# Layer 3's keys and values lead by eight tiles; expert weights and int8 weights are asked for later

## The chip, the cores and the metric

The kernel runs on one core of one Trainium2 chip. The metric is the device time of one launch in microseconds (us); less is better. A core has five engines with instruction streams of their own: PE (TensorE, the matmuls), DVE (VectorE), ACT (ScalarE), POOL (GpSimd) and SP (SyncE, which here issues most transfers). Each engine works through its own stream in order; where it needs another's result it waits on a semaphore. Transfers are issued on queues of SP, ACT or POOL and carried out by the core's 16 DMA engines.

## The reference

Four layers follow each other on x of 32 x 64 x 512 (float32), that is 2048 rows or 16 tiles of 128 rows. Each layer is `x = x + ffn(cond(x))`.

- Layer 0: every pair of 64 rows is multiplied by a matrix chosen by an index; then latent attention and a mixture of experts, one shared and 7 routed, two for each row.
- Layer 1: again a matrix chosen by an index, then a mixture of 32 experts, four for each row.
- Layer 2: a low-rank adapter chosen by an index, then a soft mixture of experts.
- Layer 3: attention against a paged cache, then an int8-quantised linear layer.

The change concerns the start of the experts in layers 0 and 1, and layer 3. In short, for layer 3:

```python
q, k, v = x @ Wq.T, x @ Wk.T, x @ Wv.T          # 32 sequences of 64 rows, two to a tile
q, k = rope(rms(q)), rope(rms(k))               # positions from kv_lens
k_blocks, v_blocks = cache with the new k, v written at their positions
p = softmax(q @ k_all.T / 16, within a window of 256 behind each position)
y = (p @ v_all) @ Wo.T
out = int8(y) @ int8(weight).T * scales + bias  # scale per row of y, per row of weight
```

and for an expert in layer 0: `silu(x @ wg) * (x @ wu) / 8 @ wd`, added with the router's weights.

## The kernel before, in words

**How the order comes about.** The program is written out as Python that records instructions; a scheduling layer may reorder the instructions of an engine, except those that are recorded as to be kept in program order. `Prog.dma` keeps its transfers in program order unless told otherwise (`later=True` is its default, while `Prog.load` passes `later=False` unless asked). Gathers (`Prog.gather`, L284) are indirect transfers issued by POOL.

**Experts of layers 0 and 1 (`Moe`).** After routing, the rows of each expert stand in slots: `C` slots for each of `E` experts (640 slots and 7 experts in layer 0; 32 experts in layer 1). The work goes in units of 320 slots, two units to a pair of five row tiles. For each pair, `rows_of` gathers five row tiles `xr` on POOL, `turn` transposes them on PE (`tp`, L924), and then `into(u)` runs the gate and up matmuls (`gu`, L943: 128x128 weights against 320 columns), the activation, and `out_of(t)` the down matmul (`y`, L962) and the write of the result `ys` on SP. The weights of an expert are one transfer of 1536 or 1538 KB into one of three buffers (`weights(e)`, `wt`). Before unit u the weights for the expert of that unit and for the next two are asked for; before unit 0 only the first two. All these transfers are on SP's queue. Since they are kept in program order, but units are only an order of recording, the third expert's transfer stands on SP ahead of the first constants of layer 3.

**Beside the experts of layer 0** runs `layer3_ahead`, a generator whose steps are taken between the tiles of the experts (`Side`). Its first step loads layer 3's constants (480.5 KB), key lengths, the block table and the int8 weights (`w_i8`, 1024 KB, L213). Later steps work out the indices of cache rows, gather the cache rows, and quantise the weights.

**Layer 3.** `units` is a list of projections: `(1, t)` is the key and value projection of tile t (L1870, 8 matmuls of 128x512), `(0, t)` the query projection. Keys and values lead by `LAG` = 5 tiles. Queries 13 to 15 (`LAST` = 3) are not in the list: they are projected by `project` (L1924, L1928) inside the attention loop, 13 at step s = -3, 14 at s = -2, 15 at s = -1. Queries 11 and 12 are in the list but are only copied there (`qlate`) and normalised and rotated later, beside the attention, as are 13 to 15. For each other unit the length of each head is worked out (ACT `sq`, DVE `ss`, POOL `r` L1970), then the rotation (DVE `n`, `tc`, POOL `ts` L1988, DVE `qkv` L1997). A key/value tile is then written to `newkv` in memory (L1897 on SP); a query tile is transposed by `heads` (PE `tp`, L1844) into `qT`. The transposed rows `xT3` are kept in `LAG` + 3 buffers, since a query comes `LAG` tiles after its keys.

`old_rows` loads cached rows into 24 buffers `kvt`; `new_rows(b)` gathers the new key/value rows of sequence b over them (three gathers on POOL for each sequence, from `newkv`, L284). These wait until all of `newkv` is written. `Attend` then works in 64 steps s (four to a tile: two pairs of head groups, two sequences): `keys` transposes the keys of step s+3 (`kp`, L2021), `scores` runs step s+2 (`sp`, L2048), `turn0` and `turn1` transpose the softmax of step s (`pT`, L2070), `values` the product with the values (`op`, L2095). Between them `out` runs the output projection of finished tiles (`y`, L2117). The first eight sequences' gathers (24) fill the 24 buffers; a later sequence first needs its buffers free and its cached rows loaded again.

Of the kernel before, what the change touches and what calls it, by code (L numbers as in the profile page):

```python
# [20 lines left out]
P = 128  # L21
B, T, D = 32, 64, 512
NT = B * T // P
# [7 lines left out]
UNIT = 320  # L31
# [367 lines left out]
class Front:  # L399
# [43 lines left out]
    def weights(self, i):  # L443

        self.asked = self.g.cond_weights(self.sb, "wc0", self.at, i) if i < NT else None
# [235 lines left out]
class Moe:  # L681
# [25 lines left out]
        self.wp = ctx.enter_context(tc.tile_pool(name=f"ew{E}", bufs=3, reuse_waits="tile"))  # L707
        self.wts, self.bds = {}, {}

    def weights(self, e):  # L710
        if e < self.E and e not in self.wts:
            t = self.wp.tile([P, self.wlen], F32, name="wt")
            self.g.dma(t, self.g.a[self.wname][e * P : (e + 1) * P, :])
            self.wts[e] = t
        return self.wts.get(e)

# [193 lines left out]
    def run(self, xs, per_tile):  # L910
# [3 lines left out]
        with ExitStack() as ctx:  # L914
# [19 lines left out]
            def into(u):  # L934
                wg, wu, _, bias = self.parts(self.weights(u * UNIT // C))
                xT = xTs[u // 2][:, :, (u % 2) * UNIT : (u % 2 + 1) * UNIT]
                hT = sb.tile([P, 2, UNIT], F32, name="hT", bufs=3)
                for ic in range(2):
                    gu = []
                    for wj in (wg, wu):  # L940
                        o = ps.tile([P, UNIT], F32, name="gu", tag="gu", bufs=4)
                        for c in range(4):
                            nc.tensor.matmul(  # L943
                                o, wj[:, c, ic * P : (ic + 1) * P], xT[:, c, :], start=c == 0, stop=c == 3
                            )
                        gu.append(o)
                    self.act(g, sb, hT[:, ic, :], *gu, None if bias is None else bias[:, ic::2])
                hTs[u] = hT
# [30 lines left out]
            for u in range(units):  # L979
                p = u // 2  # L980
                if u % 2 == 0 and p + 1 < pairs:
                    self.rows_of(p + 1)
                for e in range(3):
                    if (u * UNIT // C + e) < E:
                        self.weights(u * UNIT // C + e) if u >= 1 or e < 2 else None
                into(u)
                self.bias_of(u * UNIT // C)

                if u % 2 == 0 and p > 0:
                    for j in (2, 3, 4):  # L990
                        out_of(5 * (p - 1) + j)
                if u % 2 == 1:
                    out_of(5 * p)
                    out_of(5 * p + 1)
                    if p + 1 < pairs:
                        turn(p + 1)
# [581 lines left out]
def layer3_ahead(g, pool, w):  # L1578
# [15 lines left out]
    nc.sync.dma_start(out=ki, in_=a["kvlen"].rearrange("o b -> b o"))  # L1594
    tab = sb.tile([B, NBLK], I32, name="tabi")
    nc.sync.dma_start(out=tab, in_=a["table"])
    wt = g.load(sb, "w_i8")
    yield

    w["ridx"] = ridx = sb.tile([P, NT], I32, name="ridx")  # L1600
# [29 lines left out]
    nc.vector.tensor_scalar(slots[:, 0:KB], iota[0:B, 0:KB], s0p, None, ALU.add)  # L1630
    nc.vector.tensor_scalar(slots[:, KB:], iota[0:B, 0:5], wsp, None, ALU.add)
    blk = sb.tile([B, KB + 5], F32, name="blk")
    yield
    for j in range(KB + 5):
        hot = sb.tile([B, NBLK], F32, name="hot3", bufs=2)
# [130 lines left out]
            yield  # L1766


LAG = 5
LAST = 3  # L1770


def layer3(g, w, xs, xb):
# [3 lines left out]
    with ExitStack() as ctx:  # L1777
# [36 lines left out]
        with ExitStack() as c1:  # L1814
# [38 lines left out]
            for u in range(len(units) + 5):  # L1853
# [10 lines left out]
                if u < len(units):  # L1864
                    z, i = units[u]
                    if z:
                        turn(i + 1)
                    pp = ps.tile([P, D], F32, name="pp3", tag="pp", bufs=5)
                    for c in range(4):
                        nc.tensor.matmul(  # L1870
                            pp, xT[i][:, c, :], (w["w_kv3"] if z else wq)[:, c, :], start=c == 0, stop=c == 3
                        )
                    late = not z and i >= NT - LAG
                    out = wp.tile([P, D], F32, name=f"qlate{i}") if late else sb.tile([P, D], F32, name="qkv3", bufs=6)
                    outs.append(out)
                    if late:

                        nc.scalar.copy(out, pp)
                        slow.append((i, out))
                        held.append(None)  # L1880
                    elif z:
                        nc.scalar.copy(out[:, 256:512], pp[:, 256:512])
                        held.append((pp, out, l3_length(g, sb, pp[:, 0:256])))
                    else:
                        held.append((pp, out, l3_length(g, sb, pp)))
# [51 lines left out]
        for s in range(-3, last + 8):  # L1937
            if s == -3:
                project(NT - LAST)
            if s % 2 == 0:  # L1940

                if s >= 4:
                    for _ in range(3):
                        old_rows()
                new_rows(s // 2 + 4)
            elif s == -3:
                new_rows(2)
            for stage, at in (("keys", s + 3), ("turn0", s), ("scores", s + 2), ("turn1", s)):
                if 0 <= at <= last:
                    getattr(f, stage)(at)  # L1950
            if -3 < s < LAST - 3:
                project(NT - LAST + s + 3)
            f.out()
            if s >= 2 and s % 2 == 0:
                next(beside, None)
            if 0 <= s - 1 <= last:
                f.values(s - 1)
# [222 lines left out]
```

## Time and profile before

| what | value |
|---|---|
| median of 3 runs | 2704.14 us (2700.83 to 2704.36) |
| the profiled execution: time | 2703.36 us |
| the profiled execution: span | 2701.6 us, mean granted PE clock 0.97 |
| PE busy | 2524.0 us (93%) |
| DVE, ACT, POOL busy | 1417.6, 725.6, 852.3 us |
| first gather of layer 0's experts | 409.16 us |
| first gather of layer 1's experts | 736.41 us |
| last key/value projection of layer 3 ends | 2380.5 us |
| first value product of layer 3 | 2431.34 us |

All times are on the axis of the profiled execution's span. A line of the timeline reads: start, duration, engine, source line, operation, tile written `<-` tiles read, sizes, `x` count of instructions drawn together, and in brackets the idle time before and what ended it. A line of waits reads: engine, line, `<-` what was waited for, total us, times, longest. In windows the columns are the stretch, its length, busy time of PE, PE's weight loads, DVE, ACT and POOL with counts, granted PE clock, busy share of the DMA engines, GB/s.

### The profile page before, as it was taken

To read this page: it belongs to the slowest core of one execution; us is meant where nothing else is said; L and a number is where in the kernel's file an instruction comes from. 1 tells how busy PE (TensorE), PEld (TensorE's weight loads), DVE (VectorE), ACT (ScalarE), POOL (GpSimd) and SP (SyncE) were. 2 spreads that over 40 slices of the span, in tenths; PEclk is the share of its full clock that TensorE was granted. 3 is DMA by queue.
4 is the path that set the end of the run, shared out by engine and by line. 5 is a ranking of instruction groups with operands and counts; after the bars stand their busy time and mean duration, and the time that the engine had idled before them with its cause. 6 is when DMAs were issued, how large, how long until landed. Compare 5 with 4: busy or idle time off the path is not lost.

```text
span 2701.6 us, 42326 instructions
## 1 busy us (share of the span) xinstructions
PE 2524.0 (93%) x16508; PEld 1620.7 (60%) x16523; DVE 1417.6 (52%) x3439; ACT 725.6 (27%) x1503; POOL 852.3 (32%) x904
## 2 busy tenths in 40 slices
PE   7999998996699999996999999999999999979998
PEld 5777775563565555564666666666666665435554
DVE  4666655643744444443544445555544431647886
ACT  2444430111311121110222222222222221236664
POOL 2222214623232233213233333333233321563440
PEclk9999989997699999998999999999999999989999
DMA  2333214445656976544122222222222223423441
GB/s 98 131 126 117 88 67 169 161 147 184 222 184 219 343 256 212 209 173 176 52 73 73 81 80 72 72 72 72 72 75 70 92 63 117 158 77 111 135 136 48
DMA packets 136213, 343.58 MB, mean 127 GB/s; under 512 B 24249, under 2 KB 25049, under 8 KB 128704
## 3 DMA queue, kind: packets, MB, share of 16 engines
q1 hardware_dynamic: 100368, 245.84, 26.3%
q0 software_dynamic: 35056, 89.13, 10.9%
q10 hardware_dynamic: 576, 5.77, 0.5%
q8 instruction: 134, 2.20, 0.3%
q14 instruction: 79, 0.65, 0.1%
HBM read 247.10 MB, written 109.58 MB: 132 GB/s over the span
## 4 chain that ended last, share of the span: by engine, by line
PE 41%; DVE 9%; issue 2%; DMA 1%; ACT 1%; POOL 0%; another core or an unknown queue 0%; SPq 0%; ACTq 0%; POOLq 0%; DVEq 0%
PE out L1557 8%; PE lp L1414 7%; PE pp L1870 3%; PE gp L1546 3%; PE zp L1491 3%; PE yp L1359 2%; PE y L2117 2%; PE hp L1523 2%; PE op L2095 2%; PE pT L2070 2%; PE sp L2048 2%; DVE xt L1025 1%; PE ep L1500 1%; DVE inv L1450 1%; PE kp L2021 1%
## 5 line engine op out<-in xcount | busy, mean ns | idle before, releaser
L943 PE MATMUL gu<-xT,wt 128*128 128x320 f32 x1472 | 408.5, 434 | 0.0
L943 PEld LDWEIGHTS gu<-xT,wt 128*128 128x128 f32 x1472 | 278.7, 191 | 123.4 <-issue 16.4
L1557 PE MATMUL out<-sb_w,gT 128*128 128x512 f32 x512 | 233.5, 599 | 10.7 <-DVE nn L1394 6.6
L962 PE MATMUL y<-wt,hT 128*128 128x512 f32 (+1 forms) x552 | 240.2, 608 | 0.2 <-DVE yo L971 0.2
L1414 PEld LDWEIGHTS lp<-xnT,sb_mu 128*128 128x128 f32 x2048 | 234.8, 193 | 9.2 <-issue 6.7
L1414 PE MATMUL lp<-xnT,sb_mu 128*128 128x128 f32 x2048 | 237.8, 276 | 2.1 <-ACT xnT L254 1.3
L1491 PE MATMUL zp<-sb_w,xnT 128*128 128x512 f32 x512 | 228.6, 595 | 5.1 <-DVE z L1493 5.1
L284 POOL DMA_INDIRECT kvst<-kv,gidx x96 | 97.7, 1017 | 271.6 <-DMA oldkv<-kvst 197.5
L1550 DVE COPY gT<-gp 128x512 f32<-128x512 f32 x64 | 44.3, 692 | 248.8 <-PE gp L1546 248.4
L1557 PEld LDWEIGHTS out<-sb_w,gT 128*128 128x128 f32 x512 | 93.3, 190 | 115.7 <-issue 95.2
L1491 PEld LDWEIGHTS zp<-sb_w,xnT 128*128 128x128 f32 x512 | 93.7, 190 | 113.2 <-issue 100.0
L284 POOL DMA_INDIRECT xr<-rows,stok x115 | 110.3, 959 | 153.3 <-PE tp L924 81.8
L284 POOL DMA_INDIRECT kvt<-newkv,oidx x96 | 97.8, 1019 | 135.6 <-DMA kvt<-oldkv 70.8
L962 PEld LDWEIGHTS y<-wt,hT 128*128 128x128 f32 (+1 forms) x552 | 80.5, 172 | 98.5 <-issue 83.2
L677 POOL TENSOR_TENSOR ga<-ga,sg 128x320 f32<-128x320 f32 x64 | 55.2, 862 | 266.2 <-ACT sg L673 262.7
L284 POOL DMA_INDIRECT yk<-ys,slot x96 | 98.3, 1024 | 128.6 <-SPq L823 66.2
L1528 ACT ACTIVATE h<-hp 128x512 f32<-128x512 f32 x128 | 69.5, 594 | 217.0 <-PE hp L1523 216.8
L673 ACT ACTIVATE sg<-ga 128x320 f32<-128x320 f32 x64 | 30.0, 469 | 278.5 <-DVE ga L671 274.7
L924 PEld LDWEIGHTS tp<-sb_cst,xr 128*128 128x128 f32 x460 | 54.8, 149 | 67.4 <-issue 38.4
L1419 DVE TENSOR_TENSOR lT<-lp,cmu 128x512 f32<-128x512 f32 x64 | 43.5, 680 | 94.5 <-PE lp L1414 93.6
L971 DVE TENSOR_TENSOR yo<-y,bd 128x512 f32<-128x512 f32 (+1 forms) x96 | 66.3, 691 | 50.1 <-PE y L962 46.4
L2055 DVE CUSTOM_DVE_ANT_0 s<-sp,mask 128x336 f32<-128x336 f32 x128 | 60.8, 503 | 59.8 <-PE sp L2048 25.1
(380 smaller groups left out, 4565.0 us busy)
## 6 DMA issues: line engine op xcount, KB each, us to landing
wt<-w_e SPq DMA_DIRECT2D x32, 1538.0 KB
ys<-yo SPq DMA_DIRECT2D x115, 256.0 KB
oldkv<-kvst SPq DMA_DIRECT2D x96, 224.0 KB
kvt<-oldkv SPq DMA_DIRECT2D x96, 224.0 KB
ys<-zero SPq DMA_DIRECT2D x10, 2048.0 KB
xt<-x SPq DMA_DIRECT2D x62, 256.0 KB
x<-xt SPq DMA_DIRECT2D x48, 256.0 KB
wt<-w_e SPq DMA_DIRECT2D x7, 1536.0 KB
```

The source lines that it names most:

```text
L284: ins = self.nc.gpsimd.indirect_dma_start(out=out, out_offset=None, in_=src, in_offset=bass.IndirectOffsetOnAxis(ap=idx, axis=0), **kw)
L677: nc.gpsimd.tensor_tensor(ga, ga, sg, ALU.mult)
L943: nc.tensor.matmul(o, wj[:, c, ic * P : (ic + 1) * P], xT[:, c, :], start=c == 0, stop=c == 3)
L962: nc.tensor.matmul(y[row : row + n, :], hTs[u][:, ic, col : col + n], wd[:, ic, :], start=ic == 0, stop=ic == 1,)
L971: nc.vector.tensor_tensor(yo[r], y[r], bd[r], ALU.add)
L1414: g.first(e + c, nc.tensor.matmul(lp[:, e, :], w["mu"][:, c, (4 * q + e) * P : (4 * q + e + 1) * P], self.xnT[:, c, :], start=c == 0, stop ...
L1491: g.first(c, nc.tensor.matmul(zp, self.xnT[:, c, :], w["w1"][:, c, cols], start=c == 0, stop=c == 3))
L1528: g.pin(nc.scalar.activation(self.hs[q][b], hp[:, b], AF.Gelu))
L1546: g.first(e + b + k, nc.tensor.matmul(gp[r, e, cols], self.hs[q][b][:, e, r], self.lT[q][:, e, cols], start=True, stop=True))
L1557: g.first(e, nc.tensor.matmul(self.out, self.gTs[q][:, e, :], w["w2"][:, 4 * q + e, :], start=q + e == 0, stop=q + e == 6 and q == 3))
L1870: nc.tensor.matmul(pp, xT[i][:, c, :], (w["w_kv3"] if z else wq)[:, c, :], start=c == 0, stop=c == 3)
L2055: nc.vector.tensor_tensor_reduce(p, sps[j], self.masks[2 * i + half], -0.0625, 3.0e38, ALU.add, ALU.min, m)
```

## The change

There are three edits.

1. `Moe.weights` takes the queue as an argument. The third expert's weights (e = 2) are asked for right behind `into(0)` on ACT's queue, in both layers with experts. The test that the expert exists is left to `weights` itself.
2. In `layer3_ahead` the int8 weights are loaded two steps later, and kept in program order there.
3. In layer 3, `LAG` is 8 in place of 5: eight key/value projections run before the first query projection. A new `LATE` = 5 keeps queries 11 and 12 as the late ones of the list. `xT3` has 11 buffers in place of 8. Projections 13 and 14 are both issued at s = -3, in front of the first keys, and 15 at s = -2.

In the instruction streams as built: on SP, layer 0's third `wt` is gone from its place ahead of the constants, and the int8 weights' load stands behind three `ys` writes, in front of the fourth expert's `wt`. On ACT the third `wt` stands behind the first unit's activations, in layer 1 likewise. On DVE thirteen small operations of `layer3_ahead` stand ahead of the first `sg` (L663). On PE, queries 0 to 6 pair with keys and values 8 to 15 in layer 3's first part (query 7 follows the last key/value projection), then come queries 7 to 12 with heads 5 to 10 among them, then projections 13 and 14, nine key transposes, scores 0, projection 15, scores 1. On POOL the first eleven gathers of `kvt` stand between the `r` and `ts` of queries 7 to 10; then follow seven in a row, one `r`, and six more.

```diff
-    def weights(self, e):
+    def weights(self, e, eng=None):
         if e < self.E and e not in self.wts:
             t = self.wp.tile([P, self.wlen], F32, name="wt")
-            self.g.dma(t, self.g.a[self.wname][e * P : (e + 1) * P, :])
+            self.g.dma(t, self.g.a[self.wname][e * P : (e + 1) * P, :], eng)
...
                 for e in range(3):
-                    if (u * UNIT // C + e) < E:
-                        self.weights(u * UNIT // C + e) if u >= 1 or e < 2 else None
+                    self.weights(u * UNIT // C + e) if u >= 1 or e < 2 else None
                 into(u)
+                if u == 0:
+
+                    self.weights(2, nc.scalar)
...
     nc.sync.dma_start(out=tab, in_=a["table"])
-    wt = g.load(sb, "w_i8")
     yield
...
     blk = sb.tile([B, KB + 5], F32, name="blk")
+    wt = g.load(sb, "w_i8", later=True)
     yield
...
-LAG = 5
+LAG = 8
+LATE = 5
 LAST = 3
...
-                    late = not z and i >= NT - LAG
+                    late = not z and i >= NT - LATE
...
             if s == -3:
                 project(NT - LAST)
+                project(NT - LAST + 1)
...
-            if -3 < s < LAST - 3:
-                project(NT - LAST + s + 3)
+            if -3 < s < LAST - 4:
+                project(NT - LAST + s + 4)
```

## The prediction

> **What bounds the kernel now.** I began with the page's first two parts: TensorE (PE) is busy in 93% of the span, so an edit pays only where PE stands still. The slices show dips near 400 us and near 2420 us, which are the places that the edits touch (start of the layer 0 experts, hand-over to layer 3's attention). So I read PE's waits and its timeline there, and POOL's and SP's timelines beside them.
>
> Experts of layer 0, PE's waits from 400 to 430 us, then its timeline and SP's:
>
> ```profile
> PE tp L924 <- DMA xr<-rows,stok: 9.2, 3, 4.2
> ```
>
> ```profile
> 412.70 0.63 PE L924 MATMUL tp<-sb_cst,xr 128*128 128x128 f32 x4 [2.47 <-DMA xr<-rows,stok]
> 417.48 1.11 PE L924 MATMUL tp<-sb_cst,xr 128*128 128x128 f32 x4 [4.15 <-DMA xr<-rows,stok]
> 421.22 1.09 PE L924 MATMUL tp<-sb_cst,xr 128*128 128x128 f32 x4 [2.62 <-DMA xr<-rows,stok]
> ...
> 423.38 1.27 PE L943 MATMUL gu<-xT,wt 128*128 128x320 f32 x2
> ```
>
> ```profile
> 411.24 0.42 SPq L213 DMA_DIRECT2D wt<-w_e  x1
> 414.97 0.33 SPq L213 DMA_DIRECT2D sb_cst<-cst  x1
> ...
> 418.17 0.50 SPq L213 DMA_DIRECT2D sb_w_i<-w_i  x1
> ```
>
> PE waits for row tiles that POOL gathers from 409.16 us on, one per 1.25 us. On the same DMA engines run the third expert's weights (1536 KB), the constants (480.5 KB) and the int8 weights (1024 KB). Layer 1 does the same start with its three weights already landed; its first gather is issued at 736.41:
>
> ```profile
> 739.85 1.09 PE L924 MATMUL tp<-sb_cst,xr 128*128 128x128 f32 x4 [4.69 <-DMA xr<-rows,stok]
> 741.34 1.09 PE L924 MATMUL tp<-sb_cst,xr 128*128 128x128 f32 x4 [0.40 <-DMA xr<-rows,stok]
> ...
> 744.68 1.38 PE L943 MATMUL gu<-xT,wt 128*128 128x320 f32 x2
> ```
>
> The stretches 412 to 420 and 736 to 744 us (busy time of PE, PEld, DVE, ACT, POOL; granted clock; DMA share; GB/s) give the reason:
>
> ```profile
> 412.00:420.00 8.00, 1.74 (x8) 1.13 (x8) 1.72 (x5) 0.00 (x0) 6.17 (x7) 0.71 0.94 334
> 736.00:744.00 8.00, 3.42 (x13) 2.38 (x14) 0.82 (x2) 0.59 (x1) 5.76 (x7) 0.50 0.54 153
> ```
>
> Hand-over in layer 3, PE's timeline, the same stretches, and the chain:
>
> ```profile
> 2394.53 0.63 PE L1844 MATMUL tp<-sb_cst,qkv 128*128 128x128 f32 x4 [2.25 <-DVE qkv L1997]
> 2394.99 5.30 PE L1928 MATMUL pp<-w_q,tab 128*128 128x512 f32 x8
> ...
> 2425.73 0.82 PE L2021 MATMUL kp<-sb_cst,kvt 112*128 112x112 f32 x3 [5.50 <-ACT kT L2025]
> ...
> 2431.34 1.47 PE L2095 MATMUL op<-pTs,kvt 112*64 112x128 f32 x12
> ```
>
> ```profile
> 2415.00:2420.00 5.00, 2.07 (x5) 0.97 (x5) 2.30 (x8) 0.67 (x2) 4.37 (x4) 0.55 0.17 42
> 2420.00:2425.00 5.00, 0.24 (x2) 0.00 (x0) 0.01 (x1) 0.59 (x1) 3.91 (x4) 0.50 0.13 31
> ```
>
> ```profile
> 2418.58 5.21 another core or an unknown queue
> ```
>
> The last key/value tile's projection ends at 2380.5, its rows are written at 2391.01, and POOL then issues 24 gathers from 2393.82 to 2426.30 (1.286 us apart, one `r` of 1.68 among them). While the long run of gathers lasts, PE's releases come late (5.2 us unexplained in the chain) and PE is almost idle for ten microseconds. From op(0), the first value product at 2431.34, attention runs on PE without a gap (10.00 of 10.00 at 2440 to 2450), one unit per 3.67 us. So op(0) is the time to forecast there.
>
> **Change, part 1: third expert's weights and int8 weights in layer 0.** From the first gather to the first `gu`, layer 0 takes 423.38 - 409.16 = 14.22 us; layer 1, without the big loads, 744.68 - 736.41 = 8.27. The difference, 5.95 us, is the upper bound. What remains in the way is the 480.5 KB of constants, now issued at about 411.3 instead of 414.97: at 334 GB/s that is 1.4 us at most. The gain is 4.5 to 6; I take 5.0. Lower bound: if only the int8 weights' megabyte mattered, 1024 KB / 334 GB/s = 3 us; if the gathers in layer 0 are slow by themselves, 0. I stay near the upper end, because layer 1 is the same code, engines and shapes.
> The freed time is kept: from 430 us to 633 us PE is busy (58.6 to 60 of every 60 us), so all later work starts earlier. Moves with it: the 1536 KB now go out on ACT's queue, behind the first unit's two activations (about 422); the issue costs ACT what it costs SP, 0.42 us, and they land some 1536 / 334 = 4.6 us later, near 428 to 431, against a need at the fifth unit near 478. The cover is 45 us; if it were gone it would cost those 4.6 us. It shares the engines with the last gathers, which are for tiles PE reaches units later. On SP the int8 load now stands behind three `ys` writes and ahead of the fourth expert's weights, needed near 540; both stand queued some 80 us ahead, price 0, and at worst the megabyte's 3 us. On DVE thirteen small operations on constants come ahead of the first `sg`; their loads are issued 3.5 us earlier, so they wait less, but if they wait, `sg` waits behind them: 0 to 1 us, taken within the 5.0. POOL's gathers keep their order.
>
> The Trainium skill (Trainium Kernel Development and Optimization, and DMA: Bandwidth & Descriptors, "Issuing engines are not separate DMA queues") says that SP, ACT and POOL queues all end on the same 16 engines. That speaks against any gain from the ACT queue as such; it would give 0 for a mere change of queue. The share of 0.94 agrees, and what helps here is only the later time.
>
> **Part 2: third expert in layer 1.** Its weights were asked for at 721.83 and the page shows their landing before the gathers; PE there waits for routing. Gain 0, at best 0.5. Now they are asked for near 757, needed near 783: 26 us for a transfer of under 5. Price 0, or 5 if that cover fails.
>
> **Part 3: layer 3.** Three query projections fewer stand ahead of the last key/value tile: each is 3.43 us of matmul and 0.44 of head transposes, 3 x 3.87 = 11.6 us. So kv15 ends near 2368.9, its write goes out near 2379.4, and the first gather (2.81 later, as before) near 2382.2. The work does not vanish: the queries now follow, so on POOL the gathers stand interleaved with the last `r` (1.65) and `ts` (1.28) of queries 7 to 10. Walking POOL's new order with these durations: gather 1 to 2383.5, r9 2385.1, gather 2, ts7 2387.7, gathers 3 to 5, r10 2393.2, gather 6, ts8 2395.8, gathers 7 to 9, ts9 2400.9, gathers 10 and 11, ts10 2404.8, gathers 12 to 18 2413.8, r 2415.5, gathers 19 to 24 2423.2. Before, the last ended at 2426.30.
> On PE the last query (12) ends at 2390.4 and heads 7 at 2390.9. Then PE waits: heads 8, 9 and 10 each need a `ts` that stands behind gathers, plus 1.56 us of DVE (2392.97 to 2394.53 before). Heads 10 run at 2406.3 to 2406.8, a new stall of 14.6 us, ahead of the two projections 13 and 14. In place of it go the stalls of before: 2.25, then 0.43, 1.28, 1.26, 3.34, 5.50, 1.36 = 15.4 us. Projections 13 and 14 cost 2 x 3.44, and more after the stall: before, projection 13 took 5.30 at a clock of 0.66 after 2.25 us idle (+1.86); with a colder start I take +2.6. They end at T = 2416.3. From T to op(0) stand nine key transposes 1.0, scores 0.8, projection 15 3.45, scores 0.8, two rounds of keys, turns and scores of 2.05: 10.2, with some latency 11. So op(0) comes near 2427.3 against 2431.34, a gain of 4.0. By another road: op(0) came 5.0 after the last gather (2426.30); with the last at 2423.2 that is 2428.3, a gain of 3.0. I take 3.0. Bounds: warm and without latency, T = 2413.7 and op(0) at 2423.9, gain 7.4; with the late releases of before on the three heads (2.87 to 5.21 each in the chain, so 8.6 to 15.6), a loss of 4.6 to 11.6. The xT3 buffers only cost space.
>
> On the cold clock, TensorE: Matmul & The Clock Gate, Part 1, says half speed follows an idle window of about 3.4 us and lasts until about 3.4 us of steady work. By that rule the 6.9 us of projections 13 and 14 would cost about 3.4 more than warm, not 2.6, and the gain by PE's road would be 3.2; it speaks against putting both behind a stall.
>
> **Sum.** -5.0 + 0 - 3.0 = -8.0 against the profiled execution's 2703.36 us (2701.6 span and 1.8 around it): 2695.4. The median, 2704.14, is 0.8 above that execution, which gives 2696.
>
> **Rivals.**
> (a) Layer 3 gives nothing: the stall ahead of projection 13 (14.6) simply takes the place of the old ones (15.4), a cold start of 1 to 2 us makes up the rest. For it: the two sums are almost equal. Against: the gathers end 3 us earlier. 2704.1 - 5 = 2699.
> (b) Slower: the late releases during gather runs fall on the heads. Before, the gathers hit scores that had slack; now PE's in-order queue stands behind heads 8, 9, 10, each with its own release. With 5.2 us each layer 3 loses 11.6, less 5 from layer 0: +6.6, 2711. It decides from about 4.7 us each. For it: the 5.21 in the chain. Against: it showed only from the tenth gather in a row, and the new order has at most three in a row until ts10.
> (c) The load relief does not happen: layer 0's gathers are slow by themselves or the constants take the bandwidth. Only layer 3's 3 us: 2701.
>
> **How the numbers follow.** Forecast (both gains, 2690 to 2698.7) 0.50; (a) 0.24, (c) 0.12, (b) 0.14. A change of 0.2% is 5.4 us, about what a measurement of this kernel can tell from none: faster is under 2698.7. (a) at 2699 lies on that bound, and some four parts in ten of it fall below. Faster 0.5 + 0.10 = 0.60; same the rest of (a) and (c), 0.26; slower 0.14. The range runs from 2690 (6 and 7.4 gained) up to 2707, into (b); the forecast's own is 2690 to 2698.7.
>
> **What would show it.** Part 1: PE's wait for `xr` falls from 9.2 to near 4 us and the first `gu` comes 8 to 9.5 us after the first gather; the DMA share in these 8 us falls. Part 2: the first `gu` of layer 1 still 8.3 us after its gather. Part 3: the first `kvt` gather some 11.6 us earlier against kv0, heads 8 to 10 waiting for DVE `qkv` in three pieces of 4 to 6 us, projections 13 and 14 in one run with a clock near 0.5 at its start, op(0) 3 to 4 us earlier in the layer. I am wrong if heads come later than their `ts` plus 2 us, if scores 2 and 3 again wait 3 us and more for nothing shown, or if the gathers of layer 0 still come 3.7 us apart.

## The result, and the profile after

| what | before | changed |
|---|---|---|
| median of 20 runs | 2700.93 us (2695.87 to 2715.31) | 2698.95 us (2693.06 to 2706.03) |
| ratio of the changed kernel to the one before, 95% interval | | 0.9985 (0.9976 to 0.9994) |
| span of the profiled execution, mean granted PE clock | 2701.6 us, 0.970 | 2694.7 us, 0.973 |
| PE, DVE, ACT, POOL busy | 2524.0, 1417.6, 725.6, 852.3 us | 2523.2, 1417.9, 725.1, 853.9 us |

The changed kernel is faster by 0.15%, between 0.06% and 0.24%: about 4 us, where 8 were forecast. The spans of the two profiled executions, 6.9 us apart, say less: executions of one and the same kernel differ by some 2 us for each 0.001 of mean granted clock (last section), and these two are 0.003 apart. So stretches of the traces are compared below, each from one event to another of the same trace.

**The start of layer 0's experts.** PE's waits from 400 to 430 us of the changed kernel, then its timeline (start, duration, engine, line, operation, in brackets the idle time before and what ended it):

```profile
PE tp L924 <- DMA xr<-rows,stok: 4.8, 4, 2.4
```

```profile
415.19 0.63 PE L924 MATMUL tp<-sb_cst,xr 128*128 128x128 f32 x4 [2.40 <-DMA xr<-rows,stok]
417.21 0.83 PE L924 MATMUL tp<-sb_cst,xr 128*128 128x128 f32 x4 [1.40 <-DMA xr<-rows,stok]
418.57 2.02 PE L924 MATMUL tp<-sb_cst,xr 128*128 128x128 f32 x8 [0.53 <-DMA xr<-rows,stok]
420.44 1.44 PE L943 MATMUL gu<-xT,wt 128*128 128x320 f32 x2
422.35 1.08 PE L924 MATMUL tp<-sb_cst,xr 128*128 128x128 f32 x4 [0.48 <-DMA xr<-rows,stok]
...
443.93 1.04 PE L924 MATMUL tp<-sb_cst,xr 128*128 128x128 f32 x8
444.89 1.07 PE L962 MATMUL y<-wt,hT 128*64 128x512 f32 x2
...
448.39 1.97 PE L924 MATMUL tp<-sb_cst,xr 128*128 128x128 f32 x8 [2.42 <-DVE xT L929]
```

The windows from 412 to 420, 424 to 429 and 446 to 451 us (busy time of PE, PE's weight loads, DVE, ACT, POOL; granted clock; DMA share; GB/s), and ACT's timeline:

```profile
412.00:420.00 8.00, 3.68 (x19) 2.48 (x18) 3.21 (x9) 0.00 (x0) 6.17 (x7) 0.85 0.68 215
424.00:429.00 5.00, 5.00 (x19) 3.46 (x19) 1.56 (x14) 0.00 (x0) 3.78 (x5) 0.96 0.75 243
446.00:451.00 5.00, 2.61 (x10) 1.86 (x12) 4.20 (x9) 0.00 (x0) 2.86 (x3) 0.73 0.54 164
```

```profile
430.03 0.44 ACT L662 ACTIVATE sg<-gu 128x320 f32<-128x320 f32 x1 [19.69 <-PE gu L943]
...
433.06 0.38 ACTq L213 DMA_DIRECT2D wt<-w_e  x1
```

The first gather is issued at 411.80. PE's wait for row tiles has fallen from 9.2 to 4.8 us, the DMA share from 0.94 to 0.68, and the first `gu` comes 420.44 - 411.80 = 8.64 us after the gather instead of 14.22. But the first activation `sg` runs at 430.03, though the `gu` matmul that it needs ended 4.44 us earlier, and at 448.39 PE stands 2.42 us for a copy `xT` on DVE; before, all its waits for `xT` from 430 to 640 us were 1.0 us, now they are 3.4. The clock is at 0.50 from 419 to 424 us in both kernels; in the kernel before the window from 424 to 429 us reads

```profile
424.00:429.00 5.00, 5.00 (x20) 3.67 (x19) 1.50 (x4) 0.44 (x1) 1.95 (x3) 0.84 0.96 367
```

So the clock is full again at about 424.4 us now, 3.9 us behind the first `gu`, and was at about 425.6 us before, 2.2 us behind it.

How much of the head start is left further on, in us from the first gather:

| | first `gu` | 64th `gu` | 128th `gu` | end of layer 0's experts |
|---|---|---|---|---|
| before | 14.2 | 32.7 | 61.0 | 224.3 |
| changed | 8.6 | 28.4 | 62.3 | 226.0 |

**The start of layer 1's experts**, PE's timeline; the first gather is issued at 735.75:

```profile
739.13 1.09 PE L924 MATMUL tp<-sb_cst,xr 128*128 128x128 f32 x4 [4.63 <-DMA xr<-rows,stok]
...
744.14 1.25 PE L943 MATMUL gu<-xT,wt 128*128 128x320 f32 x2
```

Here the first `gu` stands 8.39 us behind its gather, before 8.27.

**Layer 3's hand-over**, PE's waits from 2370 to 2440 us, its timeline, and POOL's:

```profile
PE tp L1847 <- DVE qkv L2001: 14.0, 3, 6.3
```

```profile
2394.14 1.08 PE L1847 MATMUL tp<-sb_cst,qkv 128*128 128x128 f32 x4 [6.35 <-DVE qkv L2001]
...
2399.70 1.09 PE L1847 MATMUL tp<-sb_cst,qkv 128*128 128x128 f32 x4 [4.47 <-DVE qkv L2001]
...
2403.97 1.09 PE L1847 MATMUL tp<-sb_cst,qkv 128*128 128x128 f32 x4 [3.18 <-DVE qkv L2001]
2404.85 8.37 PE L1931 MATMUL pp<-w_q,tab 128*128 128x512 f32 x16
...
2423.86 0.88 PE L2099 MATMUL op<-pTs,kvt 112*64 112x128 f32 x12
```

```profile
2379.10 1.39 POOL L284 DMA_INDIRECT kvt<-newkv,oidx  x1 [2.37 <-DMA kvt<-oldkv]
...
2401.76 1.27 POOL L1992 TENSOR_TENSOR ts<-n,tab 128x512 f32<-128x512 f32 x1
...
2420.44 0.97 POOL L284 DMA_INDIRECT kvt<-newkv,oidx  x1 [0.30 <-issue]
```

Heads 8, 9 and 10 stand in front of projections 13 and 14 and wait 6.35, 4.47 and 3.18 us; the sixteen matmuls of the two projections then take 8.37 us. From the first key/value projection of the layer to op(0) it is 146.23 us, before 150.46; to the fifth value product, op(4), 160.05 against 164.88.

### The profile page after: what moved, and what is told of

Same layout as the page of the kernel before. It is cut to its first block, busy times and chain, and to the rows that moved or that the text cites. A ratio compares the mean times of both kernels' runs of the same rounds, so it can differ in the third digit from the quotient of the medians.

```text
span 2694.7 us, 42337 instructions
## 1 busy us (share of the span) xinstructions
PE 2523.2 (94%) x16508; PEld 1618.7 (60%) x16523; DVE 1417.9 (53%) x3439; ACT 725.1 (27%) x1503; POOL 853.9 (32%) x904
## 4 chain that ended last, share of the span: by engine, by line
PE 41%; DVE 10%; issue 2%; POOL 1%; DMA 1%; ACT 0%; SPq 0%; ACTq 0%; POOLq 0%; another core or an unknown queue 0%; DVEq 0%
PE out L1559 8%; PE lp L1416 7%; PE gp L1548 3%; PE pp L1873 3%; PE zp L1493 3%; PE yp L1361 2%; PE y L2121 2%; PE hp L1525 2%; PE op L2099 2%; PE pT L2074 2%; PE sp L2052 1%; DVE xt L1027 1%; PE ep L1502 1%; DVE inv L1452 1%; PE kp L2025 1%
## 5 line engine op out<-in xcount | busy, mean ns | idle before, releaser
L1570 POOL TENSOR_TENSOR xt<-xt,bc_bias 128x512 f32<-128x512 f32 x16 | 20.3, 1266 | 220.2 <-DMA x<-xt 220.2
```

## The experiments

Each was timed in five rounds against the kernel before on the same chip: twelve runs each, six for e7_pairs. The first four shared one set of runs of the kernel before (median 2695.5 us), the next four another (2694.7), the last four a third (2704.6). All ratios are to the kernel before, with 95% intervals.

**e1_layer3: part 3 alone.** The changed kernel with the loads as before.

```diff
-                if u == 0:
-                    self.weights(2, nc.scalar)
...
+    wt = g.load(sb, "w_i8")
     yield
...
-    wt = g.load(sb, "w_i8", later=True)
```

> Part 3 alone on the kernel before (LAG 8, projections 13 and 14 together, 15 at s = -2); the loads of layers 0 and 1 as before. Theory A (the change's gain is layer 3's; what layer 0 wins at its start is lost again inside its experts): op(0) comes 4 us earlier against layer 3's first key/value projection than in the kernel before (150.5 us there, 146.2 in the changed one), and the time falls by 4 us, ratio 0.9985. Theory B (both parts keep what they win, the rest is scatter): 3 to 4 us, ratio 0.9987. Theory C (layer 3's new stall of 14 us cancels its gain in undisturbed runs): ratio 1.000.

Measured: 0.9983 (0.9972 to 0.9993). From the first key/value projection to op(4) 161.13 us. The layer's gain is there without the loads; 0.9985 and 0.9987, the first two theories, are too near each other to be told apart here.

**e2_loads: parts 1 and 2 alone.** The changed kernel with layer 3 as before.

```diff
-LAG = 8
+LAG = 5
...
-                project(NT - LAST + 1)
...
-            if -3 < s < LAST - 4:
-                project(NT - LAST + s + 4)
+            if -3 < s < LAST - 3:
+                project(NT - LAST + s + 3)
```

> Parts 1 and 2 alone: third expert's and int8 weights asked for later, layer 3 as before. Theory A: first gu 8 to 9 us after the first gather (14.2 before, 8.6 in the changed kernel), but from the first gu to the end of layer 0's experts 215 to 218 us in place of 210.1, since sg starts some 4 us late behind the gathers, the block lookups on DVE pile up behind it and the transposes of the next pair wait for xT; time within 1.5 us of before, ratio 1.000. Theory B: the 5 us stay, ratio 0.998. Theory C: all of the change's gain is here, ratio 0.9985.

Measured: 1.0019 (1.0005 to 1.0032): slower. The first `gu` of layer 0 is as early as forecast, 8.6 us after its gather, but the 64th stands at 30.3 (2.4 left of 5.6), the 128th at 61.8 and the end of the experts at 225.7, later than before's 224.3. The first activation comes 4.81 us after its matmul. So the head start is real and lost within 60 us. The 5 us by which the run is slower are more than the 1.4 us that its trace shows in layer 0; the rest was not located.

**e3_fill: the stall in front of projections 13 and 14 filled.** The changed kernel with queries 13 to 15 in the list of projections, so that PE has their work instead of waiting for heads.

```diff
-                (z, i) for t in range(NT + LAG) for z, i in ((1, t), (0, t - LAG)) if 0 <= i < NT - (not z) * LAST
+                (z, i) for t in range(NT + LAG) for z, i in ((1, t), (0, t - LAG)) if 0 <= i < NT
...
-                project(NT - LAST)
-                project(NT - LAST + 1)
...
-            if -3 < s < LAST - 4:
-                project(NT - LAST + s + 4)
```

> The changed kernel with queries 13 to 15 projected in the list of projections, one ahead of each of the heads 8, 9 and 10, in place of inside the attention. If PE's stall ahead of heads 8 to 10 (14.0 us in the changed kernel) sets op(0): 10.3 us of projections move into it, op(0) comes 7 to 9.5 us earlier against the first key/value projection than in the changed kernel (146.2), and the time is 10 to 13 us under the kernel before, ratio 0.9955. If the long run of gathers with its late releases sets op(0) anyway: op(0) no more than 3 us earlier, ratio 0.9975 to 0.9985.

Measured: 1.0001 (0.9986 to 1.0015). PE's timeline of e3_fill:

```profile
2388.72 0.63 PE L1847 MATMUL tp<-sb_cst,qkv 128*128 128x128 f32 x4 [2.91 <-DVE qkv L1998]
...
2398.55 0.63 PE L1847 MATMUL tp<-sb_cst,qkv 128*128 128x128 f32 x4 [0.19 <-DVE qkv L1998]
...
2413.72 0.88 PE L2096 MATMUL op<-pTs,kvt 112*64 112x128 f32 x12
2416.08 0.51 PE L2022 MATMUL kp<-sb_cst,kvt 112*128 112x112 f32 x3 [1.49 <-issue]
```

The waits of 6.35, 4.47 and 3.18 have shrunk to 2.91 and 0.19, and op(0) comes 141.52 us after the first key/value projection, 4.7 earlier than in the changed kernel. But the last of the 24 gathers is issued only 1.6 us earlier (141.18 against 142.80 us after that projection), op(1) comes 5.9 us after op(0) instead of 2.8, and at op(4) e3_fill (158.87) is only 1.2 ahead of the changed kernel, of 10.3 us of projections moved into the gap. Neither forecast was met: 4.7 us at op(0) lie between "7 to 9.5" and "no more than 3", and the ratio lies above both. Part of the stall may have been time that the gathers need anyway; part of the gain was spent at a colder clock, which stands at 0.50 from 2405 to 2410 us and at 0.71 from 2415 to 2420, where the changed kernel has 0.75 and 1.00. How the loss divides between the two was not tested.

**e4_lookups: DVE's table lookups spread out.** In the changed kernel 26 lookups (`hot`) of `layer3_ahead` fill DVE from 432 to 446 us, just ahead of PE's wait for `xT`. Here they are kept in program order and the generator yields more often in the one place, less often in another.

```diff
-        nc.vector.scalar_tensor_tensor(
+        g.pin(nc.vector.scalar_tensor_tensor(
             hot, iota[0:B, 0:NBLK], slots[:, j : j + 1], tabf, ALU.is_equal, ALU.mult,
             accum_out=blk[:, j : j + 1],
-        )
-        if j % 8 == 7:
+        ))
+        if j % 3 == 2:
             yield
...
-        if q % 6 == 5:
+        if q % 9 == 8:
             yield
```

> The changed kernel with the 26 block lookups of layer 3 kept in program order on DVE, three to a step in place of eight (and nine of the later comparisons to a step in place of six), so that none stands ahead of the next pair's xT. Theory A: PE's waits for xT (3.4 us in layer 0) fall under 1 us, layer 0's experts take 212 us or less from the first gu to their end (217.3 in the changed kernel), the time falls 3 to 5 us under the changed kernel, ratio to before 0.997. If the lookups are not what gives the start's gain back: length and time as in the changed kernel, ratio 0.9985.

Measured: 0.9977 (0.9964 to 0.9989). From the first `gu` to the end of the experts 216.52 us, against 217.33 in the changed kernel and 210.1 before: most of what was lost is still lost. PE's wait for `xT` up to 500 us fell from 2.4 to 0.8 us, but over the whole of layer 0 from 3.4 to 3.0 only, where under 1 was expected. The ratio is a little lower than the changed kernel's, but the intervals overlap.

**e5_int8: the kernel before with the int8 load moved, nothing else.**

```diff
-    wt = g.load(sb, "w_i8")
     yield
...
+    wt = g.load(sb, "w_i8", later=True)
     yield
```

> The kernel before with part 1's second half alone: the int8 weights loaded two steps later, the third expert's weights where they were. Theory A (a sooner start of layer 0's experts is given back inside them): first gu 11 to 13.5 us after the first gather in place of 14.2, sum from the first gather to the end of the experts 223 to 226 us as before (224.3), ratio 1.000. Theory B (this half helps, the other half hurts): sum 2 us shorter, ratio 0.9993.

Measured: 1.0010 (0.9997 to 1.0023). The first `gu` comes 13.5 us after the gather, before 14.2: moving this megabyte alone frees nearly nothing, since the third expert's weights still go first. The end of the experts stands at 227.4, later than either theory had it.

**e6_third: the kernel before with the third expert's weights moved in layer 0, nothing else.**

```diff
+                if u == 0 and E == E0:
+                    self.weights(2, nc.scalar)
```

(and the queue as argument of `weights`, as in the change).

> The kernel before with the third expert's weights behind the first unit on ACT's queue in layer 0 alone; int8 weights, layer 1 and layer 3 as before. Theory A: first gu 9 to 11.5 us after the first gather, from there to the end of the experts 213 to 216 us, sum as before (224.3) within 1.5 us, ratio 1.000 to 1.001. Theory B (the loads' 1.0019 comes from this half): sum 2 us longer or more, ratio 1.0015 or more.

Measured: 1.0015 (1.0001 to 1.0030). First `gu` at 10.6 us, the 64th at 30.2, the 128th at 63.6, the end at 227.1. Here the first activation was prompt (0.04 us), and the head start of 3.6 us at the first `gu` still came to nothing; the longer sum and the ratio are those of the second theory. But the late release is there all the same, one step on: DVE's first `hT`, which also needs the up matmuls, runs 1.95 us after the last of these. e3_fill, prompt at the first activation too, shows it more plainly on DVE's timeline (its last up matmul ended at 423.09):

```profile
425.93 0.49 DVE L664 TENSOR_TENSOR hT<-gu,sg 128x320 f32<-128x320 f32 x1 [1.67 <-PE gu L943]
```

So these two kernels do not clear the late releases.

**e7_pairs: the narrow pieces of `y` kept side by side.** A `y` of 320 rows ends in a piece of 64 rows (128*64 in the profile); two such matmuls that follow each other on PE start some 7 ns apart and take 0.43 to 0.53 us together, from the first's start to the next matmul's, one alone 0.48 to 0.52. Before, 20 pairs of layer 0 stand side by side; with any of the loads' edits or the lookups' new order, 18. Here, on part 3 alone, they are kept in program order, so that all 28 pair up.

```diff
-                        nc.tensor.matmul(
+                        ins = nc.tensor.matmul(
...
+                        if j == 2:
+                            g.pin(ins)
```

> Part 3 on the kernel before, and the down matmuls of the row tile that two units share (64-column pieces, L962) kept in program order, so that the pieces of the two halves stand next to each other. In the traces a pair of such pieces starts 7 ns apart and takes 0.43 us for both, while a piece alone takes 0.43 to 0.48; of 184 pieces in both layers 76 stand alone before. If pairs share the array: 38 pairs more, 38 x 0.43 = 16 us less, less what the fixed order costs; ratio 0.992 to 0.995. If the pairing is only how the records look: ratio as part 3 alone, 0.998.

Measured: 1.0139 (1.0115 to 1.0163), a clear loss where a gain was forecast. PE's waits in e7_pairs, layer 0 from 440 to 630 us and layer 1 from 745 to 1220:

```profile
PE tp L924 <- DVE xT L929: 7.9, 7, 3.9
```

```profile
PE gu L943 <- DMA wt<-w_e: 19.0, 13, 2.7
```

The `y` matmuls did become cheaper (70.95 us of PE's busy time in layer 0 in e1_layer3, 65.08 here), but they had stood between the transposes as cover for DVE's copies, and in layer 1 PE then waited 19.0 us for expert weights, before not at all. Layer 1's experts went from 481 to 504 us. The run says what a fixed order costs here, and not what a pair is worth; by the durations a lost pair is some 1.0 - 0.5 = 0.5 us.

**e8_lag: the lead of eight tiles alone.** The kernel before with `LAG` = 8, `LATE` = 5 and 11 buffers; projections 13, 14 and 15 at their old steps, loads as before. Against the changed kernel:

```diff
                 project(NT - LAST)
-                project(NT - LAST + 1)
...
-            if -3 < s < LAST - 4:
-                project(NT - LAST + s + 4)
+            if -3 < s < LAST - 3:
+                project(NT - LAST + s + 3)
```

> The kernel before with LAG 8 and 11 xT3 buffers alone: projection 13 at s = -3, 14 at s = -2 and 15 at s = -1 as before, loads as before. If the lead of eight tiles carries the gain: the fifth value product comes 160 to 161 us after the first key/value projection (164.9 and 164.3 in the two kernels with LAG 5, 160.1 and 161.1 in those with LAG 8 and two projections together), ratio 0.9985. If the two projections in front are needed to cover something: 162.5 us or more, ratio 0.9993 or more.

Measured: 0.9996 (0.9983 to 1.0010); from the first key/value projection to op(4) 160.13 us, as with the two projections in front (159.49 to 161.38 in the other kernels with `LAG` = 8, e3_fill left out). PE's waits and timeline in e8_lag:

```profile
PE tp L1845 <- DVE qkv L1998: 14.0, 3, 6.3
```

```profile
2403.95 5.47 PE L1929 MATMUL pp<-w_q,tab 128*128 128x512 f32 x8
...
2422.95 0.88 PE L2096 MATMUL op<-pTs,kvt 112*64 112x128 f32 x12
```

The same 14.0 us in front of the same heads. The trace puts the whole gain of layer 3 on the lead; the time of the run does not confirm or deny a gain of 3 us, its interval reaches from -4.6 to +2.7.

**e9_pause: fewer gathers in a row in layer 0.** In the changed kernel POOL issues thirteen gathers without a pause from 411.80 us on. Here the second pair's gathers come behind `into(0)`, behind a small POOL operation that reads the first unit's result.

```diff
...
-                if u % 2 == 0 and p + 1 < pairs:
+                if u % 2 == 0 and p + 1 < pairs and (u or E != E0):
...
+                    if E == E0:
+                        gate = sb.tile([P, 1], F32, name="gate", bufs=1)
+                        g.pin(nc.gpsimd.tensor_scalar(gate, hTs[0][:, 0, 0:1], 1.0, None, ALU.mult))
+                        self.rows_of(1, True)
```

> The changed kernel with layer 0's gathers for the second pair of row tiles held, by one small POOL operation that reads the first unit's hT, until the first half of unit 0 is through; so POOL issues five gathers in place of thirteen in a row. If the late sg comes from PE's releases standing behind the run of gathers: ACT's first sg starts within 0.5 us of the end of the matmul it waits for (4.4 us late in the changed kernel, 4.8 and 3.4 in two more with these loads), and the experts take 213 to 215 us from the first gu in place of 217.3; ratio 0.997 to 0.998. If the lateness has another cause: still 3 us or more late, ratio as the changed kernel.

Measured: 0.9974 (0.9958 to 0.9990). POOL's and ACT's timelines and PE's waits from 409 to 500 us in e9_pause:

```profile
414.55 0.95 POOL L284 DMA_INDIRECT xr<-rows,stok  x1 [0.30 <-issue]
...
428.03 0.39 POOL L991 TENSOR_SCALAR gate<-hT 128x1 f32<-128x1 f32 x1 [12.54 <-DVE hT L664]
```

```profile
424.76 0.44 ACT L662 ACTIVATE sg<-gu 128x320 f32<-128x320 f32 x1 [16.84 <-PE gu L943]
```

```profile
PE tp L924 <- DVE xT L929: 0.4, 1, 0.4
```

After five gathers POOL is quiet, and the first activation runs 0.04 us after its matmul; PE's wait for `xT` in this stretch is 0.4 us instead of 2.4 in the changed kernel (from 430 to 640 us, 1.9 instead of 3.4). The first `hT` is prompt too (0.04 us). The mechanism is what was expected, with one reservation: the pause also empties the DMA engines (share 0.16 from 419 to 424 us, 0.73 in the changed kernel), so the run of gathers and its traffic are not told apart. But from the first `gu` to the end of the experts it is 216.24 us, 1.1 less than in the changed kernel, where 213 to 215 were expected. In this trace the clock is full again only 7.7 us behind the first `gu`, before 2.2; half of the difference, 2.8 us, is an estimate of what that cost.

**e10_both: e9_pause and e4_lookups together.** The changed kernel with the edits of both:

```diff
...
-                if u % 2 == 0 and p + 1 < pairs:
+                if u % 2 == 0 and p + 1 < pairs and (u or E != E0):
...
-        if j % 8 == 7:
+        ))
+        if j % 3 == 2:
...
```

> The pause of the gathers and the lookups kept in order, both on the changed kernel. If both stretches that eat up the sooner start are removed: first gu to end of the experts 211 to 213 us, from the first gather on 220 to 222 in place of 226.0, ratio 0.996 to 0.997. If one of them already did what there is to do: ratio as the better of the two alone.

Measured: 0.9974 (0.9959 to 0.9990). The activation is again prompt (0.04 us). The 128th `gu` stands at 58.2 us and the end at 222.8, from the first `gu` 213.53 us: in the trace half of the lost 7.2 us is back. Of the 2.7 us less than in e9_pause some 2.2, by the same estimate, go with the clock, which was full again 3.3 us behind the first `gu` instead of 7.7. The time shows no more than e9_pause alone.

**e11_again: the changed kernel once more,** with no edit, beside these two.

> The changed kernel once more, beside the others on one chip. The two parts alone gave 0.9983 and 1.0019, which multiply to 1.0002; the changed kernel gave 0.9985 on another chip. If the parts add up: 0.9995 to 1.001 here. If they help each other, or the scatter of single parts is the reason: 0.998 to 0.999.

Measured: 0.9982 (0.9968 to 0.9997), as at first (0.9985). The first activation was 6.06 us late, the head start 5.7 us at the first `gu`, 1.8 at the 64th, gone at the 128th (63.4); the end stands at 227.0.

**e12_l3look: part 3 and the lookups of e4_lookups, loads as before.** Against e1_layer3:

```diff
-        nc.vector.scalar_tensor_tensor(
+        g.pin(nc.vector.scalar_tensor_tensor(
...
-        if j % 8 == 7:
+        ))
+        if j % 3 == 2:
...
-        if q % 6 == 5:
+        if q % 9 == 8:
```

> Part 3 on the kernel before with the lookups kept in order and no change to the loads. If the loads bring nothing at the end: as the changed kernel with the lookups in order, 0.997 to 0.998. If the loads' sooner start counts once the lookups are out of the way: 0.9985 or more here, above that kernel's 0.9977.

Measured: 0.9995 (0.9980 to 1.0010). First `gu` 14.6, end 229.6 us: spreading the lookups is no gain of its own; its trace has the latest end of layer 0's experts but for e7_pairs. By the bounds set above this is the second case, in which the loads' sooner start counts once the lookups are in order. But 0.9995 and e4_lookups' 0.9977 were measured against different runs of the kernel before, and their intervals overlap, so it is not shown.

None of these is a kernel clearly better than the changed one: e4_lookups, e9_pause and e10_both all beat the kernel before, but their intervals overlap those of the changed kernel (0.9976 to 0.9994, and 0.9968 to 0.9997 in e11_again).

The layer 0 stretch over all traces, in us from the first gather; how late the first activation (`sg`) and DVE's first `hT` come after their matmuls; and how long after the first `gu` the granted clock, 0.50 there in every trace, is full again:

| kernel | first `gu` | 64th | 128th | end | `sg` late | `hT` late | clock full |
|---|---|---|---|---|---|---|---|
| before | 14.2 | 32.7 | 61.0 | 224.3 | 0.43 | 0.04 | 2.2 |
| e1_layer3 | 13.6 | 32.3 | 61.4 | 224.6 | 1.80 | 0.71 | 2.7 |
| e8_lag | 14.4 | 32.8 | 61.3 | 225.0 | 1.31 | 0.22 | 2.1 |
| changed | 8.6 | 28.4 | 62.3 | 226.0 | 4.44 | 5.23 | 3.9 |
| e11_again | 8.5 | 30.9 | 63.4 | 227.0 | 6.06 | 6.28 | 6.0 |
| e2_loads | 8.6 | 30.3 | 61.8 | 225.7 | 4.81 | 4.34 | 7.6 |
| e3_fill | 8.6 | 29.8 | 59.9 | 223.8 | 0.04 | 2.84 | 5.9 |
| e4_lookups | 9.2 | 31.0 | 60.8 | 225.7 | 3.36 | 3.61 | 7.1 |
| e9_pause | 8.5 | 30.5 | 60.8 | 224.7 | 0.04 | 0.04 | 7.7 |
| e10_both | 9.3 | 28.4 | 58.2 | 222.8 | 0.04 | 0.20 | 3.3 |
| e6_third | 10.6 | 30.2 | 63.6 | 227.1 | 0.04 | 1.95 | 3.9 |
| e5_int8 | 13.5 | 32.3 | 63.1 | 227.4 | 1.79 | 0.70 | 2.9 |
| e12_l3look | 14.6 | 32.8 | 62.6 | 229.6 | 1.66 | 0.58 | 1.7 |
| e7_pairs | 14.1 | 32.7 | 65.6 | 235.5 | 0.08 | 0.04 | 2.5 |

## Why the prediction was right or wrong

**Total.** Forecast 2696, a gain of 8.0 us or 0.3%; measured 0.15% (0.06 to 0.24), some 4 us. The sign and the range held; the sum did not. The median, 2698.95, lies just above the forecast's own range (2690 to 2698.7), and that it came so near has luck in it: the kernel before, too, came out lower, at 2700.93 with twenty runs against 2704.14 with three. By the traces the gain is made of two terms: layer 3 gives 3.2 us, layer 0 loses 1.6 (the mean end of the experts in changed, e11_again and e2_loads is 226.2 us after the first gather, in before, e1_layer3 and e8_lag 224.6). That makes -1.6 us, at the small edge of the measured -6.5 to -1.6. What makes up the rest was not located, and single traces cannot place it: from the end of layer 0's experts to layer 1's first gather, the same changed kernel took 98.0 us in one execution and 105.8 in another (e11_again). The parts measured one by one do not settle it: 0.9983 for part 3 and 1.0019 for the loads multiply to 1.0002, the changed kernel itself gave 0.9985 and 0.9982.

**Part 1: the step that failed is "The freed time is kept".** Up to the first `gu` it came as worked out, though the constants were issued 5.6 us after the first gather, about as before (5.8), and not 2.1: 8.64 us from gather to `gu` against the forecast 8 to 9.5, PE's wait for `xr` 4.8 against "near 4", the DMA share down. The gain at that point is 5.6 us where 5.0 was taken. But the forecast put it into the sum because PE "is busy" from 430 to 633 us, and a busy PE was read as a PE that cannot lose. It lost it in two steps. By the 64th `gu`, 1.3 to 3.9 us are gone (changed, e11_again, e2_loads): the fifth row tile is still awaited for 0.5 to 1.8 us, and the clock, 0.50 at the first `gu`, is full again 3.9 to 7.6 us behind it, where it was 2.1 to 2.7 us in before, e1_layer3 and e8_lag. Half of the difference to before, 0.9 to 2.7 us, is an estimate of that cost. Over all traces the time from the first to the 64th `gu` grows with it, from 18.2 us where the clock was full after 1.7 us to some 22 where it took 6 to 7.7. Between the 64th and the 128th the changed kernel needs 33.8 us where the one before needs 28.3. Of these 5.5 us, 2.42 is the wait for `xT` at 448.39; about 1.7 the reduced clock after it (0.73 in the window from 446 to 451 us, transposes 0.213 apart instead of 0.109); about 1 the two narrow pairs that no longer stand side by side. The remaining 0.4 was not placed.

Why DVE is late there: the copies `xT` queue behind the first unit's work, which waits for an activation that is 4.44 us late, and behind the lookups. DVE is busy 0.20 of the 5 us from 425.4 to 430.4, and then without a gap from 435.4 to 445.4. I had this term, as "if they wait, `sg` waits behind them: 0 to 1 us", on the wrong engine and too small. e9_pause takes the lateness away, and the wait for `xT` between 409 and 500 us goes from 2.4 to 0.4 us; that step is shown. That the late releases are the whole cause is refuted by e9_pause itself: with `sg` and `hT` both prompt it still takes 216.24 us from the first `gu` to the end, where before takes 210.1; the longer stretch at half clock is the largest item found there. e6_third and e3_fill do not test it, since their `hT` is late. A part of the loss comes with no head start at all: e5_int8 and e12_l3look start within 1 us of before and take 213.9 and 215.0 us from the first `gu` to the end, where before, e1_layer3 and e8_lag take 210.1 to 211.05. e12_l3look differs from e1_layer3 only in the order of the lookups and comparisons, so some 4 us can go with another order, by one trace of each. Which instructions cost them, and how the whole sum divides in the kernels with an early start (213.5 to 218.5 us), stays open.

The third expert's weights on ACT's queue went out at 433.06, not near 422, because the issue stands behind the late activation in ACT's order. The cover of 45 us held: PE waited for no weights. That the loads' edits gain nothing with the lookups as they were was seen directly: 1.0019, 1.0010 and 1.0015 for e2_loads, e5_int8 and e6_third, none below 1.

**Part 2** was right: layer 1's first `gu` 8.39 us after its gather (before 8.27), and no wait for weights.

**Part 3** was right in mechanism and size. Gain 3.0 forecast; the mean from the first key/value projection to op(4) is 163.8 us in the four traces with `LAG` = 5 (162.9 to 164.9) and 160.55 in the nine with `LAG` = 8 (159.5 to 161.4), so 3.2. The first gather of `kvt` came 11.5 us earlier against the first key/value projection, forecast 11.6; the stall of 14.6 us in front of the two projections came as 6.35 + 4.47 + 3.18 = 14.0; the projections took 8.37 where 6.9 + 2.6 were set, so the cold start cost 1.5; op(0) came 4.2 us earlier where PE's road gave 4.0, and 3.4 after the last gather instead of 5.0. Where it said nothing, the runs do: the projections' new place adds nothing to the lead (e8_lag 160.13), and filling the stall was worth 1.2 us at op(4) in the trace, not 14, and nothing in the time (e3_fill).

**The rivals.** (a), layer 3 gives nothing, is refuted by the traces. (b), late releases on heads 8 to 10, did not happen: each of the three starts 0.94 us after its `ts` ended, the last, heads 10, at 2403.97 after 2403.03 (2401.76 + 1.27). The same lateness did happen, in layer 0, where I had not looked for it: it was read from one place of the chain and priced only for the other run of gathers. (c) came nearest, "Only layer 3's 3 us", but for another reason: the relief did happen and did not last.

**On the clock.** The Trainium skill (TensorE: Matmul & The Clock Gate, Part 1) puts the drop to half speed after an idle window of about 3.4 us. In these traces shorter waits were followed by a lower clock, though not each time: one of 2.42 us in the changed kernel by a window at 0.73 and transposes at half pace, one of 1.93 us in e6_third by a window at 0.82; after one of 2.51 us in e11_again, the same kernel once more, the window from 446 to 451 us reads 1.00. So the measurement goes further than the page. The prediction's sum from the page's rule was off as well: 3.4 us at half speed delay the work by 1.7, not by 3.4, and measured were 1.5.

## What to carry to other kernels

Measure a head start where the work behind it has caught up, not at the first matmul: 5.6 us at the first `gu` were 1.8 to 4.3 after 64 of them and none after 128, since what follows a late result, a colder clock or another order of the same work can use it up. A stall in front of an engine's queue is only worth what the next late thing allows: 14 us of waiting in layer 3 held 1.2 us of gain in the trace and none in the time. And when a scheduler is given a new order at one place, look at every engine that it reorders for some 50 us behind.

## What the runs showed of the hardware that was not expected

**Releases from PE come late while POOL issues a long run of gathers.** In kernels with thirteen gathers in a row and early loads, the first activation came 3.4 to 6.1 us after its matmul in four of six traces (changed, e11_again, e2_loads, e4_lookups); in the other two, e3_fill and e6_third, it was prompt, but DVE's first `hT` came 2.84 and 1.95 us after its own. After five in a row both were prompt (0.20 us at most) in e9_pause and e10_both. The traffic alone does not explain it: before, the DMA share was higher (0.97 from 419 to 424 us, 0.73 in the changed kernel) and the activation 0.43 us late. Why, the runs do not tell.

**A wait of 2.4 us can already cost clock,** as said above, with about 1.7 us lost behind it in the changed kernel and nothing after a like wait in e11_again.

**An earlier start can run at half clock for longer.** In the eight traces whose first `gu` comes 8.5 to 10.6 us after the first gather, the clock is full again 3.3 to 7.7 us behind it; in the six others, at 13.5 to 14.6 us, 1.7 to 2.9 us behind it.

**Two matmuls of 128*64 that follow each other run side by side:** they start some 7 ns apart and take 0.43 to 0.53 us together, one alone 0.48 to 0.52. To force it for all of them cost 1.4% (e7_pairs). The Trainium skill (TensorE: Matmul & The Clock Gate, Part 3: Packing small matmuls) describes matmuls on parts of the array that start some 4 ns apart; the 7 ns here look like that, but no run tests it.

**The scatter of a kernel's executions goes with the clock.** Over the 35 runs of the kernel before in the first set, the time falls by 1.8 us for each 0.001 of mean granted clock, with a correlation of -0.79 (2.1 and 2.0 us in the other two sets), from 0.967 to 0.974. So a pair of single profiles says nothing of a few us of total time, and the ratios here rest on six to twenty runs of each changed kernel, never on one.
